# One written order for four engines in the second pass of a two-layer graph kernel

## The chip, the core and the metric

The kernel runs on one core of a Trainium2 chip. The core has a matrix engine (TensorE, "PE" in the profile, whose weight loads stand apart as "PEld"), a vector engine (VectorE, "DVE"), an activation engine (ScalarE, "ACT"), a general engine (GpSimd, "POOL") and a queue that here only starts transfers (SyncE, "SP"). Each engine works through its own list of instructions in the order in which the compiler or the author put them, and waits on semaphores where an instruction needs another engine's result. The metric is the device time of the whole program in microseconds (us), the median of several executions.

## What is computed

128 graphs of 64 nodes with 768 features pass through two layers, each of the form x + layer(relu(layernorm(x))). The first layer is a relational graph network; it is the first pass of the kernel and the change leaves its code alone but for one buffer. The second layer is graph attention with six heads of 128 and a gate; it is the second pass. Cut to that layer, with `feat_in` the normalized x:

```python
h = jnp.einsum('bni,hio->bhno', feat_in, W)          # 768 x 768: features of the heads
th = jnp.tanh(h)
attn_src = jnp.einsum('bhno,hoz->bhnz', th, w_src)
attn_dst = jnp.einsum('bhno,hoz->bhnz', th, w_dst)
attn = attn_src + jnp.swapaxes(attn_dst, -1, -2)     # 64 x 64 logits per graph and head
attn = jnp.where(attn >= 0, attn, 0.2 * attn)
attn = jnp.where((adj == 0)[:, None, :, :], -999.0, attn)
attn = jax.nn.softmax(attn, axis=-1)
feat_out = jnp.einsum('bhnm,bhmo->bhno', attn, h) + b
feat_out = jax.nn.elu(jnp.swapaxes(feat_out, 1, 2).reshape(B, N, -1))
gate = jax.nn.sigmoid(feat_in @ H_w.T + H_b)         # 768 x 768: the gate
out = gate * feat_out + (1.0 - gate) * feat_in
```

All of it is 32-bit float at the borders of the kernel.

## The kernel before

A tile is 128 rows: two graphs. A *pair* is two tiles, and 32 pairs pass one after the other through pass 1 and then through pass 2. In pass 2 the feature and gate products of a pair, 256 x 768 by 768 x 1536, are done in a fast scheme for 2x3 by 3x3 blocks: 15 block products in place of 18. Their left operands are sums of transposed blocks of the pair (`A_SUMS`, f1 to f11), formed by VectorE. Four PSUM accumulators, a to d, are never cleared between the products of one pair: after each product its accumulator is read into the result block that it serves, and the next product of that accumulator may start only when this read is done.

```python
PRODUCTS = (   # left, right, accumulator, first in it, result block, sign, (pass 1 only)
    ("f1", "g6", "a", True, "11", "+", False),     # 0
    ("f7", "g10", "b", True, "00", "-", False),    # 1
    ("a01", "b11", "d", True, "01", "+", True),    # 2
    ("f4", "b21", "a", False, "01", "-", False),   # 3
    ...                                            # up to 14
)
```

In pass 2 the steps of a pair are the products, two matmul calls each (`main`), and "side" steps that are traced beside them, at given places: transposes and sums of the next pair (`before`), the attention of the pair before (`behind`), and a special list for the last pair (`last`), whose feature half is computed ahead of its gate half:

```python
for ss in ((slice(0, 2),) if p < NP - 1 else (slice(0, 1), slice(1, 2))):
    ...
        product(an, bn, b, first, c, sign, c not in seen, ss)
...
def heads(t):
    th = work.tile([P, H, DO], F32, name="th")
    nc.scalar.activation(th, HS[t], AF.Tanh)
    pr = work.tile([P, 2, H, DO], F32, name="pr")
    nc.vector.tensor_mul(pr, ...)                  # by w_src and w_dst
    for h in range(H):                             # row sums: 12 activations with accum_out
        nc.scalar.activation(pr[:, 1, h, :], pr[:, 1, h, :], AF.Copy, accum_out=sd[:, 1, h : h + 1])
    ...
def rows(t): ...       # matmul, VectorE multiply, ScalarE copy: the operands of the logits
def softmax(t): ...    # logits matmul, copy_predicated, Prelu, max, six Exp
def turn_p(t): ...     # three transposes of the weights and a ScalarE copy
def attend(t): ...     # 24 matmuls of 64x64 by 64x128, six VectorE scalings
def final(t, c0=0, c1=D):
    nc.scalar.activation(e, f, AF.Exp, bias=mone)
    nc.vector.scalar_tensor_tensor(f, e, 1.0, f, op0=OP.min, op1=OP.max)
    nc.vector.scalar_tensor_tensor(f, f, 0.5, HM[t][:, c], op0=OP.mult, op1=OP.subtract)
    nc.vector.scalar_tensor_tensor(f, Z[t][:, c], 1.0, f, op0=OP.add, op1=OP.mult)
    nc.gpsimd.dma_start(of[t * P : (t + 1) * P, c], f, accum_op=OP.add)
...
for p in range(NP):
    more = [(3, lambda: finish(NP - 1))] if p == 0 else []
    if p == NP - 1:
        more += last()
    merged(main(p), own(p) + before(p + 1) + behind(p - 1) + more)
```

This trace order is only a priority: the scheduler of the tile framework decides, by its own picture of the times, in which order each engine gets its instructions. `finish(p)` closes pass 1 for a pair (layer norm of its two tiles, written to memory for pass 2), and the one of the last pair stands in pass 2's first steps:

```python
def finish(p):
    for k in range(2):
        t = 2 * p + k
        stats(X[t], to)            # VectorE bn_stats x2, aggr, add; GpSimd pow; VectorE multiply
        h = keep.tile([P, D], F32, name="hf", bufs=2)
        nc.scalar.activation(h, X[t], AF.Relu, scale=to[:, 0:1], bias=to[:, 1:2])
        nc.sync.dma_start(H1D[p][k * P : (k + 1) * P, :], h)
        nc.gpsimd.tensor_add(X[t], X[t], h)
        nc.sync.dma_start(of[t * P : (t + 1) * P, :], X[t])
        hh = keep.tile([P, D], F32, name="hh", bufs=1)
        nc.scalar.activation(hh, h, AF.Identity, scale=0.5, bias=half)
        nc.sync.dma_start(HHD[p][k * P : (k + 1) * P, :], hh)
```

Of the kernel before, what the change touches and what calls it, by code (L numbers as in the profile page):

```python
# [15 lines left out]
P = 128  # L16
# [59 lines left out]
           "b12", "v")  # L76


@with_exitstack
def kernel(  # L80
# [169 lines left out]
    hzs = [of_weights(REST + i * 2 * D, 2 * D).rearrange("p (s n) -> p s n", s=2) for i in range(4)]  # L250
    assert REST + 8 * D <= len(PLACES) * PL
# [37 lines left out]
    with ExitStack() as px:  # L289
# [276 lines left out]
# [3 lines that stand above are left out]
                to = small.tile([P, 2], F32, name="rn")  # L569
                stats(X[t], to)  # L570
                h = keep.tile([P, D], F32, name="hf", bufs=2)
                nc.scalar.activation(h, X[t], AF.Relu, scale=to[:, 0:1], bias=to[:, 1:2])  # L572
                nc.sync.dma_start(H1D[p][k * P : (k + 1) * P, :], h)
                nc.gpsimd.tensor_add(X[t], X[t], h)  # L574
                nc.sync.dma_start(of[t * P : (t + 1) * P, :], X[t])
                hh = keep.tile([P, D], F32, name="hh", bufs=1)
                nc.scalar.activation(hh, h, AF.Identity, scale=0.5, bias=half)
                nc.sync.dma_start(HHD[p][k * P : (k + 1) * P, :], hh)
# [60 lines left out]
    with ExitStack() as px:  # L639
# [3 lines left out]
        pss = px.enter_context(tc.tile_pool(name="pss1", bufs=2, space=bass.MemoryType.PSUM))  # L643
# [3 lines left out]
        def load(p):  # L647
# [4 lines left out]
            AI[p] = work.tile([P, 2, N], I32, name="ai", bufs=3)  # L652
# [3 lines left out]
        def load_x(t):  # L656
            p, k = divmod(t, 2)
            HM[t] = work.tile([P, D], F32, name="x", bufs=2)
            nc.sync.dma_start(HM[t], HHD[p][k * P : (k + 1) * P, :])

        load(0)

# [33 lines left out]
        HS, HX, Z, PB, DN = {}, {}, {}, {}, {}  # L696
        OPS = {}

        def turn(p, k, q):

            ps = pss.tile([P, 512], F32, name="ps")[:, : KQ * P].rearrange("p (a b) -> p a b", a=KQ)
            for i in range(KQ):
                kb = q * KQ + i
                nc.tensor.transpose(ps[:, i, :], H1[2 * p + k][:, kb * P : (kb + 1) * P], ident)

            a = OPS[p, f"a{k}{q}"] = (
                work.tile([P, KQ, P], F32, name="oq") if (k, q) == (1, 1) else
                work.tile([P, KQ, P], F32, name="op", bufs=17))
            nc.scalar.copy(a, ps)

        def form(p, *names):

            for n in names:
                s0, x, s1, y = A_SUMS[n]
                t = OPS[p, n] = work.tile([P, KQ, P], F32, name="op", bufs=17)
                signed(t, s0, OPS[p, x], s1, OPS[p, y])

        def main(p):

            bank = {}  # L720
            steps = []
            for k in range(2):
                t = 2 * p + k
                HS[t] = hzs[t % 4][:, 0, :].rearrange("p (h o) -> p h o", h=H)
                Z[t] = hzs[t % 4][:, 1, :]

            def read(b, c, sign, first, ss):

                k, q = int(c[0]), int(c[1])
                cols = slice(q * CQ, (q + 1) * CQ)  # L730
                to = hzs[(2 * p + k) % 4][:, ss, cols]
                ps = bank[b][:, : (ss.stop - ss.start) * CQ].rearrange("p (s n) -> p s n", n=CQ)
                op = nc.vector.tensor_add if sign == "+" else nc.vector.tensor_sub
                if not first:
                    if sign == "+":
                        op(to, ps, to)
                    else:
                        op(to, to, ps)  # L738
                    return
                if ss.start == 0:  # L740
                    nc.scalar.activation(to[:, 0], ps[:, 0], AF.Copy,
                                         scale=1.0 if sign == "+" else -1.0)
                if ss.stop == 2:
                    s = 1 - ss.start
                    if sign == "+":
                        op(to[:, s], ps[:, s], hbb[:, cols])
                    else:
                        op(to[:, s], hbb[:, cols], ps[:, s])

            def product(an, bn, b, first, c, sign, begins, ss):  # L750
                def step(q):
                    if first and q == 0:
                        bank[b] = psm.tile([P, 512], F32, name=f"pm{b}", bufs=2 if b == "a" else 1)
                    n = ss.stop - ss.start
                    nc.tensor.matmul(  # L755
                        bank[b][:, : n * CQ], OPS[p, an][:, q, :],
                        bw2[bn][:, (2 * q + ss.start) * CQ : (2 * q + ss.stop) * CQ],
                        start=(first and q == 0), stop=(q == KQ - 1), skip_group_check=True)
                    if q == KQ - 1:
                        read(b, c, sign, begins, ss)  # L760
                for q in range(KQ):
                    steps.append(lambda q=q: step(q))

            for ss in ((slice(0, 2),) if p < NP - 1 else (slice(0, 1), slice(1, 2))):
                seen = set()
                for an, bn, b, first, c, sign, _ in PRODUCTS:
                    product(an, bn, b, first, c, sign, c not in seen, ss)
                    seen.add(c)
            return steps

        def heads(t):

            th = work.tile([P, H, DO], F32, name="th")
            nc.scalar.activation(th, HS[t], AF.Tanh)
            pr = work.tile([P, 2, H, DO], F32, name="pr")
            nc.vector.tensor_mul(pr, th[:, None].to_broadcast([P, 2, H, DO]),  # L776
                                 wsd.rearrange("p s (h o) -> p s h o", h=H))
            sd = small.tile([P, 2, H], F32, name="sd")
            sg = small.tile([P, 3, H], F32, name="sg")
            for h in range(H):  # L780
                nc.scalar.activation(pr[:, 1, h, :], pr[:, 1, h, :], AF.Copy, accum_out=sd[:, 1, h : h + 1])
            for h in range(H):
                nc.scalar.activation(pr[:, 0, h, :], pr[:, 0, h, :], AF.Copy, accum_out=sg[:, 2, h : h + 1])
            nc.gpsimd.tensor_mul(sg[:, :GT, :], sd[:, 1:2, :].to_broadcast([P, GT, H]),
                                 gm[:, :, None].to_broadcast([P, GT, H]))
            sb = sdb[t % 2]
            for i in range(NPART):
                q = sb[:, :, i * H : (i + 1) * H]
                nc.gpsimd.tensor_copy(q, sg)
                if i < NPART - 1:  # L790
                    nc.gpsimd.tensor_sub(sg, sg, q)

        def swap(t):

            hx = HX[t] = work.tile([P, H, DO], F32, name="hx")
            for g in range(GT):
                nc.sync.dma_start(hx[g * N : (g + 1) * N], HS[t][(1 - g) * N : (2 - g) * N])

        def rows(t):


            ps = pss.tile([P, 512], F32, name="ps")
            nc.tensor.matmul(ps[:NR, : N + P], sdb[t % 2].rearrange("p c v -> p (c v)")[:, :NR], idr,
                             start=True, stop=True)
            nc.vector.tensor_mul(rrow[t % 2][: 2 * HB],
                                 ps[: 2 * HB, None, :N].to_broadcast([2 * HB, H, N]), de[: 2 * HB])
            nc.scalar.copy(lrow[t % 2][2 * HB :], ps[2 * HB : NR, N : N + P])

        def gate(t):

            nc.scalar.activation(Z[t], Z[t], AF.Tanh, scale=0.5)

        def softmax(t):

            p, k = divmod(t, 2)
            a = work.tile([P, H, N], F32, name="a")
            nc.gpsimd.memset(a, NEG_MASK / LEAKY)
            pl = pss.tile([P, 512], F32, name="ps")[:, : H * N].rearrange("p (h n) -> p h n", h=H)
            nc.tensor.matmul(pl, lrow[t % 2], rrow[t % 2], start=True, stop=True)

            nc.vector.copy_predicated(a, AI[p][:, k, None, :].to_broadcast([P, H, N]), pl)
            al = work.tile([P, H, N], F32, name="al", bufs=1)
            nc.scalar.activation(al, a, AF.Prelu, alpha=LEAKY)
            mx = small.tile([P, H], F32, name="mx")
            nc.vector.tensor_reduce(mx, al, AX.X, OP.max, negate=True)  # L825
            pb = PB[t] = work.tile([P, H, N], F32, name="pb")
            dn = DN[t] = small.tile([P, H], F32, name="dn")
            for h in range(H):
                nc.scalar.activation(pb[:, h, :], al[:, h, :], AF.Exp, bias=mx[:, h : h + 1],  # L829
                                     accum_out=dn[:, h : h + 1])  # L830
            nc.vector.reciprocal(dn, dn)

        PT = {}

        def turn_p(t):

            pt = PT[t] = work.tile([P, HH, P], F32, name="pT")
            ps = pss.tile([P, 512], F32, name="ps")[:, : HH * P].rearrange("p (a b) -> p a b", a=HH)
            for c in range(HH):
                nc.tensor.transpose(ps[:, c, :],  # L840
                                    PB[t][:, 2 * c : 2 * c + 2, :].rearrange("p h n -> p (h n)"), ident)
            nc.scalar.copy(pt, ps)

        FF = {}
# [149 lines left out]
```

## Time and profile before

| | |
|---|---|
| time | 2580.13 us, median of 3 (2579.05 to 2581.68) |
| span of the profiled execution | 2577.0 us, granted TensorE clock 0.993 |
| instructions | 35545 |
| pass 1 | from the start to about 1514 us |
| pass 2 | from about 1514 us to the end: 32 pairs |

The page gives the busy time of each engine over the whole span; the two passes are different kernels in effect, so what pass 2 is worth is read from queries over stretches of its own time. A busy TensorE is not one at its peak: matmul ends are modelled and overlap the next start, so the spacing of starts in the timeline is the better measure. The chain of waits follows the end of the program back to what released each step.

### The profile page before, as it was taken

Reading aid. Unit: us, or ns where it says so; the run is one execution under the profiler, and the core shown is the slowest. Engines: PE = TensorE matmul, PEld = TensorE weight load, DVE = VectorE, ACT = ScalarE, POOL = GpSimd, SP = SyncE. Lnnn points to the kernel's source line nnn. Section 1 sums busy time; section 2 is a strip of 40 time slices with the busy share of each in tenths; the row PEclk is TensorE's granted clock in tenths of the full one; section 3 lists DMA queues with packets and bytes.
Section 4 is the critical chain, followed back from the end, with each engine's and each line's share of the span. In section 5 each row is a group of like instructions: output and inputs, shape, how many; then the busy total and the mean of one; then the engine's idle time right before and its main releaser. Section 6 shows DMA issues by size and latency. Waiting matters only on the chain.

```text
span 2577.0 us, 35545 instructions
## 1 busy us (share of the span) xinstructions
PE 2489.3 (97%) x12072; PEld 1714.2 (67%) x12072; DVE 1980.3 (77%) x4130; ACT 1079.5 (42%) x3588; POOL 492.3 (19%) x801
## 2 busy tenths in 40 slices
PE   5999999999999999999999999999999999999996
PEld 4788888888888888888888864444444444444444
DVE  8977777777777777777777557888888888888887
ACT  1222222222222122222222216666666666666666
POOL 0121121211212112121121111222222222222222
PEclk8999999999999999999999999999999999999998
DMA  5122121221312212122121263444444444444433
GB/s 172 56 74 80 52 102 52 76 78 52 103 52 76 78 52 102 52 78 76 52 101 50 79 203 78 100 100 100 99 100 100 101 100 101 99 100 100 100 75 77
DMA packets 115047, 224.19 MB, mean 87 GB/s; under 512 B 36538, under 2 KB 48941, under 8 KB 114866
## 3 DMA queue, kind: packets, MB, share of 16 engines
q1 hardware_dynamic: 105208, 196.70, 23.3%
q0 software_dynamic: 9504, 25.17, 6.9%
q8 instruction: 95, 1.56, 0.3%
q14 instruction: 86, 0.70, 0.1%
q10 hardware_dynamic: 154, 0.06, 0.0%
HBM read 95.67 MB, written 100.66 MB: 76 GB/s over the span
## 4 chain that ended last, share of the span: by engine, by line
PE 71%; DVE 18%; ACT 6%; issue 4%; DMA 1%; POOL 1%; SPq 0%; POOLq 0%; DVEq 0%; ACTq 0%
PE pwa L544 19%; PE pwb L544 16%; PE pwc L544 6%; PE pma L755 6%; PE pwd L544 6%; PE pmb L755 6%; PE pb L497 5%; DVE f L861 3%; ACT pb L829 3%; DVE op L243 3%; PE pmc L755 2%; DVE pr L776 2%; DVE f L874 2%; DVE f L872 2%; DVE weights L738 1%
## 5 line engine op out<-in xcount | busy, mean ns | idle before, releaser
L544 PE MATMUL pwa<-weights,op 128*128 128x256 f32 x2304 | 542.6, 383 | 4.3 <-DVE x L536 3.1
L544 PEld LDWEIGHTS pwa<-weights,op 128*128 128x128 f32 x2304 | 423.0, 190 | 73.4 <-DVE x L536 12.0
L243 DVE TENSOR_TENSOR op<-op 128x768 f32<-128x768 f32 (+1 forms) x512 | 339.8, 683 | 156.4 <-ACT op L505 154.5
L505 ACT COPY op<-pb 128x768 f32<-128x768 f32 x160 | 124.2, 798 | 757.0 <-PE pb L497 757.0
L755 PE MATMUL pma<-weights,op 128*128 128x512 f32 (+1 forms) x792 | 381.5, 597 | 35.2 <-DVE weights L738 29.3
L544 PE MATMUL pwb<-weights,op 128*128 128x256 f32 x1536 | 372.2, 383 | 12.9 <-DVE x L538 9.5
L544 PEld LDWEIGHTS pwb<-weights,op 128*128 128x128 f32 x1536 | 285.9, 191 | 60.7 <-DVE x L538 10.3
L755 PE MATMUL pmb<-weights,op 128*128 128x512 f32 (+1 forms) x528 | 252.4, 591 | 3.6 <-DVE weights L738 3.5
L755 PEld LDWEIGHTS pma<-weights,op 128*128 128x128 f32 x792 | 137.8, 191 | 173.8 <-issue 96.4
L225 POOL TENSOR_TENSOR rn<-ve,mhalf 128x1 f32<-128x1 f32 x128 | 89.0, 695 | 530.5 <-DVE ve L224 526.9
L544 PE MATMUL pwc<-weights,op 128*128 128x256 f32 x768 | 184.9, 383 | 0.0
L544 PE MATMUL pwd<-weights,op 128*128 128x256 f32 x768 | 176.2, 379 | 0.0
L755 PEld LDWEIGHTS pmb<-weights,op 128*128 128x128 f32 x528 | 97.0, 193 | 118.4 <-issue 82.9
L218 DVE BATCH_NORM_STATS2 st<-x 128x6 f32<-128x384 f32 x256 | 136.4, 547 | 44.7 <-DMA x<-in_x_dram 43.5
L476 POOL COPY c<-cnt 128x243 bf16<-128x243 bf16 x64 | 46.2, 751 | 649.3 <-PE pb L484 602.3
L497 PE MATMUL pb<-r,h 64*128 64x192 f32 x1536 | 153.0, 339 | 7.8 <-ACT h L406 7.7
L544 PEld LDWEIGHTS pwc<-weights,op 128*128 128x128 f32 x768 | 143.2, 190 | 25.1 <-issue 7.0
L544 PEld LDWEIGHTS pwd<-weights,op 128*128 128x128 f32 x768 | 145.9, 190 | 19.8
L572 ACT ACTIVATE hf<-x,rn 128x768 f32<-128x768 f32 x64 | 65.8, 1028 | 213.7 <-DVE rn L226 213.7
L497 PEld LDWEIGHTS pb<-r,h 64*128 64x128 f32 x1536 | 124.6, 189 | 42.7 <-issue 30.5
L829 ACT ACTIVATE pb<-al,mx 128x64 f32<-128x64 f32 x384 | 128.3, 335 | 14.8 <-DVE mx L825 14.8
L574 POOL TENSOR_TENSOR x<-x,hf 128x768 f32<-128x768 f32 x64 | 115.9, 1812 | 85.4 <-ACT hf L572 85.4
(152 smaller groups left out, 4160.3 us busy)
## 6 DMA issues: line engine op xcount, KB each, us to landing
x<-in_x_dram SPq DMA_DIRECT2D x64, 384.0 KB
h<-hf SPq DMA_DIRECT2D x64, 384.0 KB
out_dram<-x SPq DMA_DIRECT2D x64, 384.0 KB
hh<-hh SPq DMA_DIRECT2D x64, 384.0 KB
h<-h SPq DMA_DIRECT2D x64, 384.0 KB
x<-hh SPq DMA_DIRECT2D x64, 384.0 KB
hx<-weights SPq DMA_DIRECT2D x128, 192.0 KB
out_dram<-f POOLq DMA_DIRECT2D x62, 384.0 KB, 4.9
```

The costliest lines, as they stand in the source:

```text
L218: ins = nc.vector.bn_stats(st[:, i, :], src[:, i * HALF : (i + 1) * HALF])
L225: nc.gpsimd.tensor_tensor(to[:, 0:1], ve, mhalf, op=OP.pow)
L243: return (nc.vector.tensor_add if s1 == "+" else nc.vector.tensor_sub)(to, x, y)
L497: nc.tensor.matmul(ps[:, g, i * 3 * N : (i + 1) * 3 * N], H0[t][s, kb * P : (kb + 1) * P], rts[p % 2][s, k].rearrange("p s n -> p (s n)"), ...
L505: nc.scalar.copy(a.rearrange("p h s (g n) -> p g (h s) n", g=GT), ps[:, :, : 6 * N].rearrange("p g (x n) -> p g x n", n=N))
L544: nc.tensor.matmul(bank[b][:, :CQ], OPS[p, an][:, q, s, :], bw[bn][:, (s * KQ + q) * CQ : (s * KQ + q + 1) * CQ], start=(first and q == s ...
L572: nc.scalar.activation(h, X[t], AF.Relu, scale=to[:, 0:1], bias=to[:, 1:2])
L574: nc.gpsimd.tensor_add(X[t], X[t], h)
L755: nc.tensor.matmul(bank[b][:, : n * CQ], OPS[p, an][:, q, :], bw2[bn][:, (2 * q + ss.start) * CQ : (2 * q + ss.stop) * CQ], start=(first a ...
L776: nc.vector.tensor_mul(pr, th[:, None].to_broadcast([P, 2, H, DO]), wsd.rearrange("p s (h o) -> p s h o", h=H))
L829: nc.scalar.activation(pb[:, h, :], al[:, h, :], AF.Exp, bias=mx[:, h : h + 1], accum_out=dn[:, h : h + 1])
L861: nc.vector.scalar_tensor_tensor(FF[t][:, h * DO : (h + 1) * DO], po[h % 2][:, h // 2, :], DN[t][:, h : h + 1], bb, op0=OP.mult, op1=OP.add)
```

## The change

Pass 2 no longer leaves the order to the scheduler. The helpers are cut into single steps (a transpose `T`, its copy `C`, a sum `F`, half a product `P7.0`, the read of a product `R7`, the ScalarE part of a read `RA7`, and the steps of the attention of tile 0 or 1 of the pair, such as `th1`, `mul0`, `exp0.1`), and all 136 steps of a pair stand in one written order. A step with `/1`, `/2` or `/3` belongs to the pair that began one, two or three rounds earlier, so that a round of 136 steps works on up to four pairs, and a pair is spread over its own round and up to three more. `manual_schedule` holds TensorE, VectorE, ScalarE and GpSimd to the traced order; transfers started by SyncE are not held. The aim is that TensorE finds each operand and each accumulator ready when it comes to it.

Beside the order: a third PSUM buffer for the small matmuls; two more buffers for features and gate of a tile, so that three pairs can be open; sums and transposed blocks in buffers by name, five of them double; `pr` in one buffer, the inputs `x` in three, `ai` in four; `hh` of pass 1 shares the two buffers of `hf`. The last pair is no longer split into feature and gate halves, and its tail has no list of its own: after the last products, the rounds go on with what is left in them.

```diff
+ORDER = """
+Ta00 Ca00 R8/1 Ta12 P7.0/1 f1.1/3 tr0/2 Ta01 P9.0/1 Ta11 P7.1/1 RA7/1 chain1/2 R7/1 Ca12 P9.1/1
+Ca01 P11.1/1 f0.2/3 rows1/2 P10.0/1 R9/1 rrow1/2 Ca11 exp0.0/2 Ta10 P2.0 lrow1/2 Ca10 P10.1/1
+exp0.1/2 log1/2 P12.0/1 Ff1 Ta02 turnp0/2 P12.1/1 f1.2/3 P0.0 R11/1 R10/1 th0/1 Ca02 P13.0/1
+P2.1 Ff8 cp1/2 mul0/1 Ff2 dma1/3 R12/1 Ff5 pre1/2 pT0/2 P0.1 Ff3 sum0.1/1 Ff7 P14.0/1 sum0.0/1
+RA0 P13.1/1 memset0/1 Ff9 P14.1/1 R2 att0/2 sum0.2/1 tr1/2 Ff4 rec0/2 P5.0 R0 R13/1 dma0/3 Ff6
+sum0.3/1 RA14/1 R14/1 exp1.0/2 ev0.1/2 k0/1 P3.0 chain0/1 Ff10 P1.0 exp1.1/2 th1/1 P3.1 ev0.0/2
+turnp1/2 RA2 Ff11 e0/2 P1.1 P8.0 mul1/1 RA1 R1 P5.1 g1/1 pT1/2 rows0/1 R3 P4.0 lrow0/1 P6.0
+f0.0/2 g0/1 att1/2 sum1.2/1 rec1/2 rrow0/1 f0.1/2 sum1.0/1 sum1.3/1 RA5 ev1.1/2 log0/1 swap1/1
+sum1.1/1 swap0/1 P6.1 R5 ev1.0/2 e1/2 P4.1 P8.1 k1/1 R4 cp0/1 pre0/1 memset1/1 R6 P11.0 f1.0/2
+""".split()
...
+    NHZ = 6
...
-                hh = keep.tile([P, D], F32, name="hh", bufs=1)
+                hh = keep.tile([P, D], F32, name="hh", tag="hf", bufs=2)
...
-        pss = px.enter_context(tc.tile_pool(name="pss1", bufs=2, space=bass.MemoryType.PSUM))
+        pss = px.enter_context(tc.tile_pool(name="pss1", bufs=3, space=bass.MemoryType.PSUM))
...
+        hzs += [wb.tile([P, 2, D], F32, name=f"hz{i}") for i in range(4, NHZ)]
...
+        def place(p, n):
+            return work.tile([P, KQ, P], F32, name=f"op_{n}",
+                             bufs=2 if n in ("a11", "f2", "f5", "f8", "f10") else 1)
...
-            for ss in ((slice(0, 2),) if p < NP - 1 else (slice(0, 1), slice(1, 2))):
...
+            PR[t] = work.tile([P, 2, H, DO], F32, name="pr", bufs=1)
...
-        for p in range(NP):
-            more = [(3, lambda: finish(NP - 1))] if p == 0 else []
-            if p == NP - 1:
-                more += last()
-            merged(main(p), own(p) + before(p + 1) + behind(p - 1) + more)
+        order = [(n, int(k or 0)) for n, _, k in (x.partition("/") for x in ORDER)]
+        px.enter_context(tc.manual_schedule(engines={
+            mybir.EngineType.PE, mybir.EngineType.DVE, mybir.EngineType.Activation,
+            mybir.EngineType.Pool}))
+        for i in range(min(k for _, k in order), NP + max(k for _, k in order)):
+            if i >= 0:
+                load(i + 1)
+            for j, (n, k) in enumerate(order):
+                if i == 0 and j == len(order) // 4:
+                    finish(NP - 1)
+                if 0 <= i - k < NP:
+                    step(n, i - k)
```

The arithmetic is the same step for step; only the last pair's products are wider, 512 columns at once in place of twice 256.

## Prediction

> **What bounds the kernel now.** I read the page's busy times first, then busy time by stretches of pass 2, then TensorE's timeline over one pair, then who waited for whom.
>
> ```profile
> PE 2489.3 (97%) x12072; PEld 1714.2 (67%) x12072; DVE 1980.3 (77%) x4130; ACT 1079.5 (42%) x3588; POOL 492.3 (19%) x801
> ```
>
> ```profile
> 1500.00:1540.00 40.00, 36.17 (x131) 22.23 (x130) 23.71 (x49) 8.73 (x19) 9.39 (x23) 0.96 0.47 162
> ...
> 1800.00:1900.00 100.00, 96.94 (x401) 43.91 (x400) 82.74 (x171) 69.91 (x292) 22.68 (x49) 1.00 0.44 102
> ...
> 2500.00:2577.00 77.00, 53.79 (x328) 35.66 (x326) 57.70 (x127) 47.23 (x201) 15.93 (x35) 0.87 0.37 72
> ```
>
> The columns of the stretches are length, busy PE, PEld, DVE, ACT, POOL, clock, DMA share, GB/s. TensorE looks full (97%) in the steady part, with VectorE second (83%). The timeline says how full; this is the start of one pair and the end of its round:
>
> ```profile
> 1872.78 1.98 PE L755 MATMUL pma<-weights,op 128*128 128x512 f32 x4 [1.02 <-DVE weights L738]
> 1874.60 1.88 PE L755 MATMUL pmb<-weights,op 128*128 128x512 f32 x4
> 1876.32 0.25 PE L803 MATMUL ps<-idr,sdb 128*82 128x192 bf16 x1
> 1876.40 1.91 PE L755 MATMUL pma<-weights,op 128*128 128x512 f32 x4
> ...
> 1900.43 1.88 PE L755 MATMUL pma<-weights,op 128*128 128x512 f32 x4
> 1902.15 1.88 PE L755 MATMUL pmd<-weights,op 128*128 128x512 f32 x4
> ```
>
> Four product matmuls that follow one another take 1.72 us from start to start (1874.60 to 1876.32), 0.43 each; their "busy" 1.88 overlaps the next. The chain of waits gives the period: the same matmul begins a pair at 1614.58 and at 1646.84, so 32.26 us. What TensorE must do in one, by start spacing in that timeline: 60 product matmuls x 0.43 = 25.8; 12 transposes x 0.11 (four from 1891.73 to 1892.17) = 1.3; 6 transposes of weights x 0.11 = 0.7; two attention blocks 0.88 + 0.82, and 0.10 after each because the first product group behind it takes 1.82 in place of 1.72, = 1.9; two logits x 0.17 and two rows x 0.11 = 0.6. Sum: 30.2 us. So each period loses 2.0 us, and these are its waits over 29 pairs (1582 to 2518 us), TensorE's first and then its weight loads':
>
> ```profile
> PE pma L755 <- DVE weights L738: 29.3, 29, 1.0
> ...
> PEld pma L755 <- DVE weights L738: 53.3, 29, 1.9
> PEld ps L857 <- ACT pT L842: 44.0, 58, 0.8
> ...
> PEld L803 <- POOL sdb L789: 23.5, 29, 1.1
> PEld L819 <- ACT lrow L807: 22.8, 29, 0.9
> PEld pmb L755 <- DVE weights L748: 22.2, 30, 0.8
> ```
>
> One bubble of 1.0 us per pair is bare: an accumulator is read late, because VectorE has a three-step `final` in front of the read. The rest, about 0.9, is weight loads that come too late by a tenth here and there. All of it is order, not work.
>
> **What the Trainium skill says.** "Perfetto Trace Analysis", Identifying the Most-Contended Engine: matmul busy time does not tell how close a kernel is to its limit. The trace agrees: 97% busy, yet 2.0 of 32.26 us (6%) are lost. "PSUM — Partial Sum Buffer", Engine vs sequencer instructions: the queues of ScalarE, VectorE and GpSimd are strictly first in, first out. The trace agrees at the start of pass 2: VectorE waits 1.70 us for a constant's transfer at 1520.9 with ready sums behind it, and TensorE waits for one of those. "TensorE: Matmul & The Clock Gate", Part 1: an idle TensorE drops to half clock, and it takes microseconds of work to get back. The trace agrees: after its 3.39 us of idle time at 1521.4 two groups of four take 2.57 and 2.83 us in place of 1.72, so 1.9 us are lost, and the clock of that stretch is 0.96.
>
> ```profile
> 1522.61 0.66 DVE L668 TENSOR_SCALAR bb<-bb 128x128 f32<-128x128 f32 x1 [1.70 <-DMA bb<-in_b_att_dram]
> ```
>
> ```profile
> 1524.79 2.57 PE L755 MATMUL pma<-weights,op 128*128 128x512 f32 x4 [3.39 <-DVE weights L746]
> 1527.15 3.03 PE L755 MATMUL pmb<-weights,op 128*128 128x512 f32 x4
> ```
>
> **Part 1, the steady rounds.** Nothing is removed from TensorE: the same 30.2 us per round. I laid each engine's steps of one round end to end in the written order, with start spacings from the steady timelines: reads 0.60 (0.34 the first of a block), sums 0.34, the big multiply 1.68, scalings 0.26 a head, `f` 0.87, `exp` 0.33 a head, row sums 0.29, tanh 0.75, `e` 0.85. Totals: VectorE 25.8, ScalarE 20.9, GpSimd 6 to 9 of the 30.2. Then I asked at each accumulator and operand when its producer is done, letting a step begin only 0.3 us after the matmul that it reads. With TensorE's round starting at 0:
> - P8.1 of the last round ends at -0.9, R4 is done at -0.8, and P7.0, its accumulator's next, begins at 0.4: 1.2 us to spare. P9.0 begins at 1.5, R6 is done at 0.3: 1.2.
> - R7 (P7.1 ends at 3.5) is done at 4.1, P10.0 begins at 5.3; R12 at 12.4, P14.0 at 13.9; R1 at 22.7, P4.0 at 23.9.
> - `rows1` at 5.2 needs a PSUM buffer that Ca12 frees at 4.3 (0.9, the least I found) and `chain1`, done by 3.3 even where GpSimd is slow. `turnp0` at 9.3 needs `exp0.1`, done at 7.9; `att1` at 25.6 needs pT1 from 23.7.
>
> So no step in the loop is late, and VectorE has some 4 us of its own to spare. This is what removes the 1.0 us bubble and most weight-load waits. I give the round 0.2 for what such a table can't see: 30.4 us, 1.86 less than now.
>
> **Part 2, the head.** Before, pass 2 starts at 1513.7 and the third pair's products at 1582.4; by then TensorE has done 58.5 us of work (two pairs' products 51.6, three pairs' transposes 3.9, one pair's attention 3.1), so 10 us are lost. After, round 0 has only its own pair's steps: twelve transposes and P2, P0 (4 x 0.86) bring TensorE to about 1518.9. Then it needs f3, which needs Ff5, which needs the copy Ca02; and in ScalarE's fixed order Ca02 stands behind `finish` of the last pair, both tiles. Before, the first tile was finished inside pass 1 (its relu at 1511.3); now it can't start ahead of round 0. GpSimd's constants run until 1518.6 (that is the trace of before without the two memsets that move). Then: pow 0.6, VectorE 0.2, relu 1.0 (1520.5), add 1.8, second pow, relu of the second tile from about 1524, since its buffer now waits for the store of the first (before, a store of this kind landed 3.0 us after issue: `hh` issued at 1430.90, its next writer released at 1433.9), `hh` from 1526, Ca02 by 1527.3, Ff5 and Ff3 by 1528.2. TensorE idles some 9 us, then does the other 13 half products, 11.2 us, plus 2 for the cold clock: round 0 ends at 1541.4. Round 1 has no attention matmuls: 25.8 + 1.3 + 0.3 = 27.4, ends at 1569. Lost in all about 13 us; 3 worse than before.
>
> **Part 3, the tail.** Rounds 2 to 31 end at 1569 + 30 x 30.4 = 2481. Round 32 has the last pair's 13 half products and the attention of pair 30. P14.0 comes 1.3 late, as R12 stands behind the big multiply and TensorE has little to fill with; the last product ends 13.2 after 2481. From there the tile 1 of the last pair: RA14 and the two `exp1` and tanh ahead in ScalarE's order 3.4, multiply 1.7, ScalarE's five other steps before the sums 1.1, twelve row sums 3.6, GpSimd 2.3, rows to logits 2.6, choose, Prelu, maximum 2.2, `exp1` 2.1, transposes, copy and attention 2.9 (the copy behind `e0`), scalings with `f0.1` among them 1.9, `e1` 1.0, and the last VectorE steps of both tiles with one store, 4.6: 29.4; a second store 0.9. Before, the last store was handed out by 2569.13 and the program ended at 2577.0, 7.9 us later:
>
> ```profile
> 2568.27 0.86 POOL out_dram L875
> 2569.13 0.89 POOLq L990
> ```
>
> So 2481 + 13.2 + 30.3 + 7.9 = 2532.4, against 2577.0 of the profile: 44.6 less. In the old tail the last pair's gate half filled TensorE while the feature half went through its attention; that is given up, and costs some 10 us of the 30 x 1.86 = 56 that the rounds bring, with the 3 of the head. In pass 1 the shared `hh` buffer makes a relu wait for a store; ScalarE is 1 or 2 tenths busy there, and I put 0 for it. Time: 2580.1 - 44.6 = 2535.
>
> **Rivals.** (a) *VectorE becomes the bound.* A fixed order with 25.8 of 30.2 us on VectorE leaves little for waits; every late semaphore shifts all behind it. For it: VectorE is 83% busy already. Against it: the least slack in the table is 0.9 us, and VectorE's waits fall where it has room. A round of 31.3 would give 2562. (b) *The ends eat the gain.* `finish` in the chain and a tail without the split: if both cost 10 more than I put, 2555. For it: the last stretch before already has TensorE at 54 of 77 us. (c) *The order is perfect and the ends are cheap*: 30.2 a round, the head no worse than before and the tail 3 shorter: 6 + 3 + 3 less, 2523. (d) *Transfers in SyncE's queue* block (swaps and loads are not in the written order): before, loads ran rounds ahead; I expect nothing.
>
> **Range and chances.** (c) and a half-way (a) or (b) span 2520 to 2556; the lower side is a floor set by TensorE's work, so the upper side is longer. 2% is at 2528.5: reached only if most of (c) holds, 0.3. Slower by over 2% would need a round of 33.6 us, more than now ((2631.7 - 2535) / 30 = 3.2 above 30.4): 0.03. Within 2%: 0.67.
>
> **What would show each step.** The period in the chain or timeline: 30.2 to 30.6; the `pma <- DVE` wait gone from TensorE's list; VectorE's busy share in the steady part near 88%. Head: a TensorE gap of 6 to 10 us at about 1519 to 1528 that a ScalarE copy behind `finish` ends. Tail: about 43 us between the last round's end and the last store. Wrong it would be if the round is over 31, with a VectorE or GpSimd wait repeated in each round, or if pass 1 ends later than 1514.

## The result, and the profile after

| | before | after |
|---|---|---|
| time, median | 2580.39 us (2579.05 to 2581.68) | 2537.03 us (2535.85 to 2538.78) |
| ratio | | 0.9833, 95% interval 0.9816 to 0.985 |
| span of the profiled execution | 2577.0 | 2536.2 |
| one round of pass 2 | 32.26 | 30.22 |

The predicted time was 2535, with 2520 to 2556 as its range. The time is inside, 2 us off, and the ratio lies within 2%, to which I had given 0.67. But three terms of the sum missed: the rounds by 5 us in one direction, the tail by 6 and the head by 3 in the other.

First the page of the kernel after, its busy times:

```profile
PE 2460.0 (97%) x12012; PEld 1713.6 (68%) x12012; DVE 1983.1 (78%) x4115; ACT 1073.5 (42%) x3586; POOL 438.3 (17%) x799
```

The shares are what they were. The same stretches as before, the last one up to the program's end, show more (length, busy PE, PEld, DVE, ACT, POOL, clock, DMA share, GB/s):

```profile
1500.00:1540.00 40.00, 29.89 (x112) 19.63 (x111) 21.16 (x43) 7.17 (x14) 8.42 (x22) 0.87 0.52 179
1800.00:1900.00 100.00, 100.00 (x444) 47.75 (x448) 87.06 (x179) 74.46 (x315) 16.10 (x52) 1.00 0.42 101
2500.00:2536.00 36.00, 6.15 (x56) 3.71 (x56) 16.18 (x33) 10.91 (x46) 7.39 (x11) 0.50 0.37 66
```

The middle is full: TensorE is busy all of 100 us. Both ends are emptier than before: the head has 29.9 us of TensorE in place of 36.2 and a clock of 0.87 in place of 0.96, and the last 36 us are a chain of other engines at half clock. In the list of waits TensorE has not one entry from 1580 to 2460 us. The first transposes of two rounds that follow one another give the period, 30.22 us:

```profile
1571.77 0.60 PE L721 MATMUL ps<-ident,h 128*128 128x128 f32 x4
...
1601.99 0.60 PE L721 MATMUL ps<-ident,h 128*128 128x128 f32 x4
```

The chain of waits of the whole program, by engine, says the same. First before, then now:

```profile
PE 71%; DVE 18%; ACT 6%; issue 4%; DMA 1%; POOL 1%; SPq 0%; POOLq 0%; DVEq 0%; ACTq 0%
PE 93%; DVE 2%; DMA 2%; issue 2%; POOL 1%; ACT 0%; SPq 0%; POOLq 0%; DVEq 0%; ACTq 0%
```

The head, on TensorE's timeline:

```profile
1519.56 1.02 PE L745 MATMUL pma<-weights,op_f 128*128 128x512 f32 x2
1530.64 2.08 PE L745 MATMUL pmc<-weights,op_f 128*128 128x512 f32 x2 [10.06 <-DVE op_f L258]
1532.51 1.91 PE L745 MATMUL pma<-weights,op_f 128*128 128x512 f32 x2
1534.21 1.31 PE L745 MATMUL pmb<-weights,op_f 128*128 128x512 f32 x2
1535.36 1.02 PE L745 MATMUL pma<-weights,op_f 128*128 128x512 f32 x2
```

TensorE stands for 10.06 us; then three groups of two start 1.87, 1.70 and 1.15 apart in place of 0.86: 2.1 more. The releaser named is a VectorE sum, but its operand comes from ScalarE, and ScalarE's timeline says what stood in front:

```profile
1525.61 1.03 ACT L588 ACTIVATE hf<-x,rn 128x768 f32<-128x768 f32 x1 [1.70 <-DVE rn L241]
1528.60 0.93 ACT L593 ACTIVATE hh<-hf,half 128x768 f32<-128x768 f32 x1 [1.96 <-DMA hh<-hh]
1529.44 0.35 ACT L732 COPY op_a<-ps 128x256 f32<-128x256 f32 x1
```

The copy at 1529.44 is Ca02. Both tiles of `finish` stand ahead of it, and the second waits 1.96 us for a store out of the shared buffer.

To compare kernels below I take pass 2 by itself: from its first transposes on TensorE (1513.72 before, 1515.11 after) to the end of the span. What is left of it after 30 periods I call its *ends*. Before: 1063.3 = 30 x 32.26 + 95.5. After: 1021.1 = 30 x 30.22 + 114.5. So the rounds bring 61.2 us and the ends cost 19.0.

### The profile page after: what moved, and what is told of

Read it like the earlier page. It is cut to its first block, busy times and chain, and to the rows that moved or that the text cites. A ratio compares the mean times of both kernels' runs of the same rounds, so it can differ in the third digit from the quotient of the medians.

```text
span 2536.2 us, 35252 instructions
## 1 busy us (share of the span) xinstructions
PE 2460.0 (97%) x12012; PEld 1713.6 (68%) x12012; DVE 1983.1 (78%) x4115; ACT 1073.5 (42%) x3586; POOL 438.3 (17%) x799
## 4 chain that ended last, share of the span: by engine, by line
PE 93%; DVE 2%; DMA 2%; issue 2%; POOL 1%; ACT 0%; SPq 0%; POOLq 0%; DVEq 0%; ACTq 0%
PE pwa L560 19%; PE pwb L560 16%; PE pma L745 13%; PE pmb L745 11%; PE pwc L560 7%; PE pwd L560 6%; PE pb L513 5%; PE pmc L745 5%; PE pmd L745 4%; PE ps L888 2%; PE ps L721 2%; PE pwd L544 1%; PE ps L870 1%; PE ps L839 1%; DVE weights L258 0%
## 5 line engine op out<-in xcount | busy, mean ns | idle before, releaser
L258 DVE TENSOR_TENSOR op<-op 128x768 f32<-128x768 f32 x256 | 238.9, 953 | 156.0 <-ACT op L521 156.0
L745 PE MATMUL pma<-weights,op_f 128*128 128x512 f32 x640 | 318.0, 594 | 1.2 <-DVE weights L774 1.2
L797 ACT ACTIVATE pr<-pr 128x128 f32<-128x128 f32 x768 | 225.2, 295 | 24.2 <-DVE pr L787 24.2
L745 PE MATMUL pmb<-weights,op_f 128*128 128x512 f32 x384 | 197.4, 596 | 0.0
L745 PEld LDWEIGHTS pma<-weights,op_f 128*128 128x128 f32 x640 | 115.9, 191 | 120.3 <-issue 108.6
L240 POOL TENSOR_TENSOR rn<-ve,mhalf 128x1 f32<-128x1 f32 x128 | 106.9, 835 | 468.3 <-DVE ve L239 462.9
L745 PE MATMUL pmc<-weights,op_f 128*128 128x512 f32 x256 | 135.0, 609 | 10.3 <-DVE op_f L258 10.1
L797 ACT ACTIVATION_READ_ACCUMULATOR pr<-pr 128x1 f32 x768 | 144.1, 188 | 0.0
```

What stands on the lines that cost most here:

```text
L240: nc.gpsimd.tensor_tensor(to[:, 0:1], ve, mhalf, op=OP.pow)
L258: return (nc.vector.tensor_add if s1 == "+" else nc.vector.tensor_sub)(to, x, y)
L745: nc.tensor.matmul(bank[p, b], OPS[p, an][:, q, :], bw2[bn][:, 2 * q * CQ : 2 * (q + 1) * CQ], start=(first and q == 0), stop=(q == KQ - 1 ...
L797: nc.scalar.activation(PR[t][:, j, h, :], PR[t][:, j, h, :], AF.Copy, accum_out=to)
```

## Experiments

The time is the median where there are several executions; e2, e4, e8, e9, e15 and e16 ran once. Period and ends are from the one profiled execution, the ends worked out as above. The period repeats from round to round, but the ends of one execution can be off by a few us: e17's profile is of its fastest execution, 4.1 us below its median, and e12's of its slowest, 2.0 above.

| kernel | time | period | ends |
|---|---|---|---|
| before | 2580.4 | 32.26 | 95.5 |
| after | 2537.0 | 30.22 | 114.5 |
| e1_finish_free | 2530.0 | 30.22 | 106.9 |
| e2_order_free | 2531.4 | 30.58 | 98.8 |
| e4_r4_late | 2585.5 | 31.84 | 113.6 |
| e8_before_pss3 | 2567.7 | 31.94 | 93.7 |
| e9_before_buffers | 2582.2 | 32.48 | 91.4 |
| e15_free_pss2 | 2548.8 | 31.08 | 101.1 |
| e16_two_less | 2444.0 | 27.23 | 110.9 |
| e10_head | 2532.2 | 30.22 | 108.6 |
| e12_tail_free | 2524.0 | 30.22 | 102.0 |
| e13_tail_free_f3 | 2523.1 | 30.22 | 100.5 |
| e14_head_first | 2524.1 | 30.22 | 100.4 |
| e17_head_late | 2526.1 | 30.22 | 100.3 |

My theory was that holding the engines to an order in which every step has some slack takes away the waits of the rounds, and that holding is what costs at the ends. The rivals: the buffers bring the gain; or the written order brings it as a mere priority.

**e2_order_free**: the written order is traced, but nothing is held to it.

```diff
-        px.enter_context(tc.manual_schedule(engines={
-            mybir.EngineType.PE, mybir.EngineType.DVE, mybir.EngineType.Activation,
-            mybir.EngineType.Pool}))
```

> All buffers and steps as after, traced in the same order, but no engine is held to it: the scheduler of the framework places the instructions. Theory (the held order brings the 30.22 us): the period rises to 31 to 33 us, with waits of TensorE back in each round, and the time is above 2555. Rival (the third PSUM buffer, the three open pairs and the finer steps bring it): the period stays at 30.2 to 30.4 and the time at 2537 or less, since the closing of pass 1 is free too.

Measured: 2531.4 us, period 30.58. The half of the theory that speaks of the rounds fell. Without the hold the rounds keep 1.68 of the 2.04 us, and the ends are 15.7 us cheaper than in the kernel after, so that in this one execution the kernel without the hold is the faster one. The missing 0.36 us lie at one place: the product P4.0 starts some 0.36 us after `rows0` in each round, where the kernel after has 0.08, and its two matmuls then take 0.96 in place of 0.89. Its weight load comes late, since it waits for R1, the read of its accumulator (TensorE's weight loads, 28 rounds):

```profile
PEld pmb L745 <- DVE weights L774: 12.2, 18, 0.7
...
PEld pmb L745 <- DVE hz L774: 7.0, 10, 1.0
```

The scheduler has put the step `f0.0`, 0.96 us long, ahead of R1 on VectorE; the written order has R1 first.

**e8_before_pss3**: the kernel before with a third small PSUM buffer, nothing else.

```diff
-        pss = px.enter_context(tc.tile_pool(name="pss1", bufs=2, space=bass.MemoryType.PSUM))
+        pss = px.enter_context(tc.tile_pool(name="pss1", bufs=3, space=bass.MemoryType.PSUM))
```

> The kernel before with a third PSUM buffer for the small matmuls, nothing else. Theory (order): the period stays within 0.3 of 32.26, time 2570 to 2585. Rival (PSUM buffers were what the small matmuls and so the rounds waited for): the period falls below 31.5 and the time below 2555.

Measured: 2567.7 us, period 31.94: 0.32 less than before, at the edge of what I gave it. The waits of 1.0 us in each pair for the read of an accumulator shrink from 29.3 us in all to 5.5, and others open:

```profile
PE ps L704 <- ACT op L709: 11.5, 29, 0.4
PE pma L755 <- DVE weights L738: 5.5, 29, 1.0
```

**e9_before_buffers**: the kernel before with all the buffers of the kernel after.

```diff
+    NHZ = 6
...
-                hh = keep.tile([P, D], F32, name="hh", bufs=1)
+                hh = keep.tile([P, D], F32, name="hh", tag="hf", bufs=2)
...
+        pss = px.enter_context(tc.tile_pool(name="pss1", bufs=3, space=bass.MemoryType.PSUM))
...
+            AI[p] = work.tile([P, 2, N], I32, name="ai", bufs=4)
...
+            HM[t] = work.tile([P, D], F32, name="x", bufs=3)
...
+        def place(n):
+            return work.tile([P, KQ, P], F32, name=f"op_{n}",
+                             bufs=2 if n in ("a11", "f2", "f5", "f8", "f10") else 1)
...
+            pr = work.tile([P, 2, H, DO], F32, name="pr", bufs=1)
```

> The kernel before, its trace order and its coarse helpers kept, with all the buffers of the kernel after (three small PSUM buffers, six feature and gate buffers, sums and blocks by name, one pr, three x, four ai, hh with hf). If the written trace order and its fine steps bring what is left of the 1.68 us per round that a written but unheld order gave: period 31.7 or more, time 2560 or more. If the buffers bring it: period 30.8 or less, time 2537 or less.

Measured: 2582.2 us; longer and shorter rounds alternate, and 32.48 is their mean. More buffers bring nothing to the old trace order, and take the 0.32 of e8 back: the wait for an accumulator's read is there again, 26 times between 1582 and 2440 us, which is once a round:

```profile
PE pma L760 <- DVE weights L743: 13.9, 17, 1.6
PE pma L760 <- DVE hz L743: 8.4, 9, 1.6
```

**e15_free_pss2**: e2_order_free with two small PSUM buffers.

```diff
-        pss = px.enter_context(tc.tile_pool(name="pss1", bufs=3, space=bass.MemoryType.PSUM))
+        pss = px.enter_context(tc.tile_pool(name="pss1", bufs=2, space=bass.MemoryType.PSUM))
```

> As e2_order_free (written trace order, not held), with two small PSUM buffers in place of three. Before with three gave 31.94 a round in place of 32.26. If the written order with its fine steps does nearly all by itself: period 30.6 to 31.0. If the order is worth what it is only with the third buffer: 31.4 or more.

Measured: 31.08, between the two cases and just past the first. So the 2.04 us come in three parts, if taken in this sequence: 1.18 from the fine steps in the written order (with the other buffers), 0.50 from the third PSUM buffer on top of it, 0.36 from the hold. How much of the 1.18 is the order, and how much the cutting into finer steps, is not separated.

**e4_r4_late**: the read R4, which my table gave 1.2 us to spare ahead of P7.0, is moved behind R6 and `f1.0` in VectorE's order.

```diff
-... P8.1 k1/1 R4 cp0/1 pre0/1 memset1/1 R6 P11.0 f1.0/2
+... P8.1 k1/1 cp0/1 pre0/1 memset1/1 R6 P11.0 f1.0/2 R4
```

> In the written order only the read R4 moves behind f1.0, the three-step final's first, as in the kernel before. Theory (a round's length is set by TensorE as long as every slack is positive; the slack of R4 against P7.0 is 1.2 us, and it is used up through att1, ev1.1, R5, ev1.0, e1, f1.0, R4): start of P7.0 to start of att1 25.1, attention 0.9, and 0.3 + 0.8 + 0.3 + 0.8 + 1.0 + 0.95 + 0.75 behind it, 30.95, plus 0.1 for a matmul after a drained array: period 31.05 (30.9 to 31.2), one wait of 0.7 to 0.9 per round at the first matmul of P7, and 2560 (2556 to 2565) in all. Rival (VectorE's own room of 4 us takes up such a move, since its total stays 25.8): period 30.2 and time 2537.

Measured: 31.84 and 2585.5 us; 30 x 1.62 = 48.6 is the whole difference from the kernel after. One step out of place in 136 takes back more than the change brings. The wait is the one expected, once in each round:

```profile
2049.09 1.12 PE L745 MATMUL pmb<-weights,op_f 128*128 128x512 f32 x2 [1.35 <-DVE weights L774]
2080.93 1.13 PE L745 MATMUL pmb<-weights,op_f 128*128 128x512 f32 x2 [1.35 <-DVE hz L774]
```

But it is 0.8 longer than expected, so R4 has only about half of the slack in my table: in the kernel after it ends at 2055.20, 0.53 ahead of P7.0 at 2055.73. VectorE's timeline of the kernel after has a wait that I had not laid into it: the read R5 stands 0.70 us for its ScalarE half, RA5, which is behind a run of row sums, and everything behind R5 is that much later.

```profile
2053.41 0.42 DVE L774 TENSOR_TENSOR hz<-weights,pmc 128x256 f32<-128x256 f32 x1 [0.70 <-ACT hz L761]
```

**e16_two_less**: the kernel after with the matmuls of P13 and P14 left out; their accumulators are still read, so the feature and gate blocks lack two terms.

```diff
+            if k in (13, 14):
+                return
             nc.tensor.matmul(bank[p, b], OPS[p, an][:, q, :], ...)
```

> The kernel after, with the matmuls of the products P13 and P14 left out (their accumulators are still read, so the output is another). TensorE's work falls by 3.44 us, to 26.78. If TensorE's own work is all that sets 30.22: period 26.8, and the time falls by about 31.5 x 3.44 = 108, to 2429. If VectorE (25.8 us of steps by my sum) or the chain of one of the reads comes up first: 27.3 to 28.5, with a wait that recurs in each round.

Measured: 27.23 and 2444.0 us. Of TensorE's 3.44 us 2.99 come off the period. That lies between my two cases, closer to the second: TensorE's own work sets 30.22, and the next bound keeps the last 0.45. VectorE is busy 95.05 us of 100, and TensorE has one short wait for its read of an accumulator in each round:

```profile
1800.00:1900.00 100.00, 99.30 (x441) 46.93 (x440) 95.05 (x201) 80.84 (x353) 18.43 (x60) 1.00 0.48 115
```

```profile
1828.05 1.13 PE L747 MATMUL pma<-weights,op_f 128*128 128x512 f32 x2 [0.17 <-DVE hz L774]
```

This matmul starts 1.30 us after the group ahead of it, where 0.96 is usual behind the attention's matmuls, and takes 0.96 in place of 0.86 itself: together 0.44.

Now the ends.

**e1_finish_free**: `finish` of the last pair traced ahead of the held steps.

```diff
+        finish(NP - 1)
         px.enter_context(tc.manual_schedule(engines={...}))
...
-                if i == 0 and j == len(order) // 4:
-                    finish(NP - 1)
```

> Only the closing of pass 1's last pair is taken out of the held order (traced ahead of it, so that the scheduler places it). Theory (the TensorE gap of 10.06 us at 1520 us comes from that closing, in ScalarE's and VectorE's fixed order ahead of the copy Ca02 and the sums): TensorE resumes at about 1521.5 in place of 1530.64 and has no slow matmuls after it (they cost 2.1), so about 10 us less: 2527 (2524 to 2530), and the period stays 30.22. Rival (the gap is the wait for the constants' transfer, which VectorE takes in order, or for pass 1's buffers to come free): the gap stays over 6 us and the time over 2533.

Measured: 2530.0 us (2529.14 to 2530.38), at the upper edge of what I gave it; ends 7.6 less. The gap of 10.06 is gone; two small ones are left, with slow groups behind them:

```profile
1520.06 1.12 PE L745 MATMUL pmc<-weights,op_f 128*128 128x512 f32 x2 [0.76 <-DVE op_f L258]
1523.49 2.07 PE L745 MATMUL pma<-weights,op_f 128*128 128x512 f32 x2 [2.30 <-DVE weights L772]
```

Just ahead of the read that ends the second gap, VectorE spent 1.81 us on an addition to `bb`, 128x128, the attention's bias `b` (the expectations call it the gate's):

```profile
1520.63 1.81 DVE L685 TENSOR_SCALAR bb<-bb 128x128 f32<-128x128 f32 x1
```

I took it for the wait for the bias's transfer.

**e10_head**: e1 with that addition in round 1.

```diff
-        nc.vector.tensor_scalar(bb, bb, 1.0, None, op0=OP.add)
...
+            if i == 1:
+                nc.vector.tensor_scalar(bb, bb, 1.0, None, op0=OP.add)
```

> finish(NP - 1) ahead of the held region, and VectorE's addition to the gate bias moved from the head to round 1. If the 2.30 us gap of the head with finish freed is the wait for the bias transfer in VectorE's fixed order: 3 to 4 us (the gap and part of the cold clock behind it) below e1_finish_free's 2530.0, about 2526. If another step of the head is as late: 2529 to 2530.

Measured: 2532.2 us (2529.87 to 2532.57), nothing gained. The addition is gone from the head, and another instruction takes its time. VectorE's timeline, then GpSimd's:

```profile
1522.63 0.42 DVE L771 TENSOR_TENSOR weights<-pmd,weights 128x256 f32<-128x256 f32 x1
1522.96 1.70 DVE L258 TENSOR_TENSOR op_f<-op_f,op_a 128x256 f32<-128x256 f32 x1
1524.58 0.41 DVE L771 TENSOR_TENSOR weights<-pma,weights 128x256 f32<-128x256 f32 x1
```

```profile
1522.56 1.82 POOL L590 TENSOR_TENSOR x<-x,hf 128x768 f32<-128x768 f32 x1 [1.38 <-ACT hf L588]
```

A sum that takes 0.42 elsewhere took 1.70, and the next instruction starts 0.20 us after GpSimd's addition of the 128x768 tile ends. The read at 1522.63, one of whose inputs is in PSUM, ran inside that addition at its usual 0.42.

The bias's addition itself settles that it was not the transfer. In e1 GpSimd's addition starts at 1520.53 and the bias's 0.10 later. In e2_order_free it starts 0.61 later (GpSimd, then VectorE):

```profile
1521.01 1.82 POOL L590 TENSOR_TENSOR x<-x,hf 128x768 f32<-128x768 f32 x1 [1.39 <-ACT hf L588]
1521.62 1.30 DVE L685 TENSOR_SCALAR bb<-bb 128x128 f32<-128x128 f32 x1 [0.46 <-DMA bb<-in_b_att_dram]
```

The wait for the transfer is the idle 0.46 ahead of it; the addition then takes 1.30. In the kernel before GpSimd's addition runs from 1521.38 to 1523.19, and the bias's starts 1.23 into it and takes 0.66. In all three it ends 0.08 or 0.09 us after GpSimd's addition, wherever it began. In the kernel after nothing of GpSimd runs beside it, and it takes 0.23.

The Trainium skill, "SBUF — State Buffer", section "Who interferes with whom", has a rule that fits: a VectorE instruction with two SBUF inputs contends with a GpSimd instruction that reads SBUF, as its second input comes through the interface they share. The traces agree with it: the sum (two SBUF inputs) is held up, the read (one) is not. The bias's addition has one SBUF input and is held up too, so this rule alone does not cover it.

**e12_tail_free**: e10 with the rounds behind the last pair's own left to the scheduler.

```diff
-        px.enter_context(tc.manual_schedule(engines={...}))
+        held = px.enter_context(ExitStack())
+        held.enter_context(tc.manual_schedule(engines={...}))
...
+            if i == NP:
+                held.close()
```

> As e10_head, with the rounds behind the last pair's own out of the held region (the scheduler orders them), the 32 rounds held. If what the unheld order gained at its ends (17 us) lies as much in the tail as in the head: period 30.22 and 6 to 9 us below e10_head, about 2518. If the tail's length is its chain whatever the order: as e10_head, within 2.

Measured: 2524.0 us (2522.25 to 2525.99), 8 below e10's median; ends 6.6 less than e10's, the period untouched.

**e13_tail_free_f3**: e12 with three output buffers and one for the tanh.

```diff
-            TH[t] = work.tile([P, H, DO], F32, name="th")
+            TH[t] = work.tile([P, H, DO], F32, name="th", bufs=1)
-                FF[t] = work.tile([P, D], F32, name="f")
+                FF[t] = work.tile([P, D], F32, name="f", bufs=3)
```

> As e12_tail_free, with three buffers for the output tile f and one for the tanh (memory is full otherwise). The tail waited for the store of pair 30 to leave one of two f buffers (1.64 us of VectorE in the kernel after). If that wait is on the path: 1.5 to 3.5 us below e12_tail_free, about 2516, unless the single tanh buffer makes a wait per round (period over 30.3). If it is hidden: as e12_tail_free.

Measured: 2523.1 us (2522.19 to 2523.43), within e12's spread. From the last regular round's first `e` to the end of the span it is 61.3 us against 61.6: the wait for the store is hidden once the tail is not held. The rest of the 1.5 between their ends lies in the head, where TensorE's slow groups happened to end earlier.

**e14_head_first**: e13 with `finish` of the last pair ahead of GpSimd's constants in the trace.

```diff
+        finish(NP - 1)
         load(0)
...
-        finish(NP - 1)
```

> As e13_tail_free_f3, with finish(NP - 1) traced ahead of GpSimd's constants of pass 2. In e10_head VectorE waited 2.46 us in the head for GpSimd's power, which stands behind those constants, with the sums that TensorE needs behind it. If that is the wait that took the place of the one e10_head removed: its two gaps in the head (1.06 and 1.83 us) shrink below 1 us together, the cold clock behind them mostly goes, and the time is 3 to 5 us below e13_tail_free_f3's 2523.05, about 2519. If not: within 1 of it.

Measured: 2524.1 us (2523.45 to 2524.39), a miss: the two gaps are still 1.09 and 1.83, and GpSimd still works its constants off ahead of the power of the layer norm (`pow` in `stats`). They are ready first, and here the order is the scheduler's.

**e17_head_late**: e13 with the constants and GpSimd's last addition moved to the start of round 1.

```diff
+                if t == 2 * NP - 1:
+                    deferred.append(rest)      # GpSimd's addition and its store
...
+            if i == 1:
+                constants()
+                deferred[0]()
```

> As e13_tail_free_f3, with GpSimd's constants of pass 2 and its last addition of pass 1 (the second tile of the last pair, 128x768) moved from the head to round 1. In e10_head, e13 and e14 a VectorE sum that takes 0.42 us elsewhere took 1.70, beside that addition of 1.82 us on GpSimd, and the sum ended 0.06 us from the addition's end; in e1_finish_free it was the gate bias that took 1.81 beside it. If GpSimd holds VectorE up there, and not a transfer: the sum takes 0.42, TensorE's second gap in the head (1.83 us) goes, and with the constants out of the way of the power the first one (about 1.1) too, with most of the cold clock's 3: 4 to 6 us below e13's 2523.05, about 2518. If it is something else in VectorE's list: the slow sum stays, 2522 to 2523.

Measured: 2526.1 us (2521.98 to 2527.47), no gain, and the edit did not do what it was for. Round 0 has no GpSimd step in the head, so the first GpSimd steps of round 1 start as soon as the engine is free, and that is in the head. GpSimd's and VectorE's timelines are as before:

```profile
1520.35 1.82 POOL L593 TENSOR_TENSOR x<-x,hf 128x768 f32<-128x768 f32 x1 [1.38 <-ACT hf L590]
```

```profile
1520.75 1.70 DVE L258 TENSOR_TENSOR op_f<-op_f,op_a 128x256 f32<-128x256 f32 x1
```

A place in an order is no start time. No kernel here runs the slow sum without that addition beside it, so what moving the addition away would bring stays open. My estimate is 3 to 5 us: the gap of 1.83 and the slow groups behind it, which stand 1.6 (e17) to 3.1 us (e10) over their usual spacing.

The lowest median is that of e13_tail_free_f3, with e12 and e14 within 1 us: 2523.1 us, ratio to before 0.9782 (0.9767 to 0.9796), 14 us below the kernel after.

## Why the prediction came out right, and where it did not

- **The floor of a round.** TensorE's 30.2 us by start spacings: the period is 30.22. The 0.2 that I added for what the table can't see was not needed, so the rounds bring 61.2 in place of 55.8. e16 confirms the floor from the other side.
- **The table of slack.** Right in its verdict, no step is late, but not in its numbers: R4 has about half of its 1.2 us, since the table left out VectorE's wait of 0.7 for RA5. This did no harm only because some slack was left.
- **"All of it is order, not work."** Right, but it is the order of the trace: 1.18 of 2.04 come from it and its finer steps, without hold and third buffer. I had put the gain down to the fixed order as a whole and had given the third buffer nothing; it is worth 0.50 within the written order.
- **VectorE's share**, 88% expected, 87.06 measured. Rival (a) did not come; e16 shows that a read on VectorE is the next bound, some 3 us further down. Rival (d), SyncE's queue, left no wait in the rounds.
- **The head.** The mechanism was right, step for step: Ca02 behind both tiles of `finish`, the second tile behind a store. Ca02 ended at 1529.8 where I had 1527.3. All of the 2.5 is there at the first power already, which starts at 1521.09 and not at 1518.6: 1.4 because pass 2 began later, and 1.1 because VectorE waits 2.12 us for the bias's transfer ahead of the layer norm's steps. I had read this wait off the kernel before (1.70) and then left it out of the sum. From the power to the end of Ca02 it is 8.7 us, as in the sum. One wait inside it I had not seen: the first tile's `hh` was ready at 1523.92, but SyncE handed out its store at 1525.29, behind a store that waited for GpSimd's addition. Round 1 begins at 1543.9 (1541.4 predicted). e1 gives what holding `finish` costs: 7.6 us, where I had put 3 for the whole head against the kernel before. A reading was slightly wrong too: in the kernel before, the two slow groups behind the idle 3.39 us took 2.36 and 2.87 from start to start, so 1.8 was lost there and not 1.9.
- **The start of pass 2.** I gave 0 for the shared `hh` buffer and called an end of pass 1 past 1514 a sign against me. It was 1515.11. But over the kernels that share this buffer and have the same code in pass 1 it lies between 1513.32 and 1515.58, so the 1.4 can't be put down to the change.
- **The tail.** The term that failed: from the start of round 32 (about 2478.4) to the end of the span it is 57.8 us, where the sum had 51.4. Three of its steps were too short. GpSimd's chain took 4.1 in place of 2.3:

```profile
2502.74 1.03 POOL L810 TENSOR_TENSOR sg<-sg,sdb 128x18 f32<-128x18 f32 x1
2503.83 0.91 POOL L808 CAST sdb<-sg 128x18 bf16<-128x18 f32 x1
2504.82 0.23 POOL L810 TENSOR_TENSOR sg<-sg,sdb 128x18 f32<-128x18 f32 x1
```

  The last scalings waited for the store of a pair before, which I had not counted (VectorE, ahead of `ev0`):

```profile
2513.74 1.64 DVE L898 SCALAR_TENSOR_TENSOR f<-ps,dn,bb 128x128 f32<-128x128 f32 x6 [3.81 <-DMA out_dram<-f]
```

  and as the copy for the second tile's attention stands behind `e0` in ScalarE's fixed order (that I had), this delay passed on to TensorE:

```profile
2516.77 0.47 PE L888 MATMUL ps<-weights,pT 64*64 64x128 f32 x1 [4.28 <-ACT pT L875]
```

  From the end of the last `exp1` to the second tile's scalings it is 6.5 us, where the sum had 2.9. And from the last store's hand-out to the end it is 9.3 in place of 7.9. The 7.9 was itself misread: it runs from 2569.13, where the hand-out of the last store starts, and the sum counts that hand-out once more; from its end the kernel before takes 7.0.

  e12 shows how much of this the hold makes: with the tail not held its ends are 6.6 us shorter than e10's. The scalings wait 1.23 for the store in place of 4.03, the second tile's copy no longer stands behind `e0` (TensorE waits 0.57 for it in place of 4.49), and from the last hand-out to the end it is 7.4 in place of 9.2. GpSimd's chain is not part of it: it takes 4.1 in e12 too. Rival (b), the ends eat the gain, was right by some 9 us of its 20.

So +5.4 from the rounds stands against -6.4 in the tail and -2.8 in the head (round 2 begins at 1571.8, where I had 1569). The profiled span, 2536.2, is 3.8 above the sum's 2532.4, and the median came within 2 us. That closeness is luck: the errors cancelled, and two of the three are larger than what is left.

## What to carry to other kernels

Write the order of a pipelined loop out in small steps and trace it so: as a priority, with the buffers of the change, it gave 1.68 of 2.04 us a round here, and a third small PSUM buffer was worth more with it than without. Hold the engines to it only where the loop is periodic, and keep prologue and drain out of the held region: freeing both took 13 us off (e12 against the kernel after), more than the hold's 0.36 x 30 = 11 brings, and the two together are 7 us below the kernel without any hold (e2, run once). When a VectorE instruction is several times its usual length, look at GpSimd's timeline before at the transfers: a wait for a transfer stood in the idle time ahead of the instruction here, not in its length.

## What was not expected of the hardware

Short GpSimd steps on 18 columns take 0.20 to 0.23 us, and 0.91 to 1.03 in the kernel after where VectorE runs a 128x768 instruction with two SBUF inputs beside them: the step at 2502.74 above stands beside

```profile
2502.73 0.96 DVE L916 SCALAR_TENSOR_TENSOR f<-e,f 128x768 f32<-128x768 f32 x1 [1.33 <-ACT e L909]
2503.72 0.96 DVE L918 SCALAR_TENSOR_TENSOR f<-f,x 128x768 f32<-128x768 f32 x1
```

and the one at 2503.83 beside the next. In the head it is the other way round: GpSimd's addition of 1.82 us stretches a VectorE sum from 0.42 to 1.70. In these cases the one that had started first kept the other out. GpSimd's spans in the profile are rough, but VectorE's lengths beside them fit: near the usual in the tail (0.96), four times the usual in the head (1.70).
